# Four vision layers on one Trainium2 core: the selective scan under a written order of slots, with the exponentials in SBUF and the skip term on TensorE

## Chip, cores and metric

One core of a Trainium2 chip. The metric is the device time of one launch in microseconds (us). The engines are called PE (matrix multiplication), DVE (vector), ACT (activation functions), POOL (general purpose) and SP, which here only issues DMAs. All data is fp32.

## What is computed

Four layers run one after the other on 8 images of 384 channels and 32 x 32 pixels (1024 tokens): a Mamba block (layer 0), a Mamba block with a channel gate and an MLP (layer 1), seven depthwise convolutions merged into one 13 x 13 (layer 2), and a pointwise plus a depthwise convolution with GELU (layer 3). The change touches the Mamba block, which both layers 0 and 1 call. Its core, cut from the reference:

```python
u = silu(conv1d(xin) + conv_b)                      # 768 channels, 4 taps
dt_lo, Bm, Cm = split(u @ x_proj_w.T)               # 24, 16 and 16 columns
delta = softplus(dt_lo @ dt_proj_w.T + dt_proj_b)   # the step sizes
def step(h, inp):                                   # h: 768 channels x 16 states
    dt_t, u_t, B_t, C_t = inp
    dA = jnp.exp(dt_t[..., None] * A)
    h = h * dA + (dt_t * u_t)[..., None] * B_t[:, None, :]
    y = jnp.einsum('bdn,bn->bd', h, C_t)
    return (h, y)
...
y = ys + u * D                                      # the skip term
y = y * silu(z)
out = y @ out_proj_w.T                              # and the residual x is added
```

## The kernel before

**Tiling.** `mamba` walks over 16 units: image b = 0 to 7, half 0 or 1 of its 1024 tokens (T = 512 tokens). The 768 channels are six chunks d of 128. The scan has 16 states a channel, so a chunk has 2048 rows of 512 tokens; a tile of 128 partitions holds 32 channels x 4 states, and a work item handles two such tiles. Eight items (n = 0 to 7) make a chunk, 48 a unit, 768 a layer. Half 1 starts its scans from the `state` that half 0 left.

**One item** (`scan`, L273 to L295). POOL multiplies `B` (spread over the partitions) with `ur`, the repeated step size times u, into `dbu` in SBUF (L278; three buffers). ACT writes two exponentials of 512 columns into `h`, a tile in PSUM (L284; two buffers). DVE runs two scans of 512 columns over them (L288): each reads the exponentials from `h` and the addends from `dbu` and writes its result over `h`. In half 0 a small copy saves the last column (L290). DVE multiplies both with `C` into `hc` in SBUF (L292), and PE folds the states with two narrow matmuls of a 0/1 matrix into `acc` in PSUM (L295).

**The end of a chunk.** DVE forms `u * D + acc` (L296) and multiplies it with `zs`, the silu of z, from SBUF (L297).

**Step sizes.** `step_in` and `step_out` (L235 to L267) make delta and delta * u of a chunk: PE (L238), five passes on ACT, three on POOL (L253, L254, L256) and one on DVE (L255). Both tiles are written to DRAM (`dd`, `uu`) and read back repeated four times over the partitions, in eight DMAs of 128 KB for each (L265, `rdd`, `ruu`, three buffers each). They are issued inside the loop one chunk ahead: the step sizes of chunk d + 1 in items 0 and 1 of chunk d.

**The other work of a unit** is put into the items' places too (`fill`, L333 to L358): the gates z of this unit; the load, layer norm, input products, convolution (four diagonal products, L197) and silu of the next one; then its `ranks` (L216), which write B and C to DRAM and read them back spread. `back` (L299) forms the output products and adds the residual, in layer 1 after a gate on POOL (L307).

**Order.** Only ACT runs in the order that is written (`manual_schedule(engines={ACT})`, L317). The order on PE, DVE, POOL and SP is chosen by the scheduler of the language from the data dependences and its own estimates. A tile with n buffers makes its writer wait until the readers of the n-th tile before are through. Each engine runs its own queue strictly in order.

Of the kernel before, what the change touches and what calls it, by code (L numbers as in the profile page):

```python
# [9 lines left out]
F32 = mybir.dt.float32  # L10
AF = mybir.ActivationFunctionType
ALU = mybir.AluOpType
# [82 lines left out]

def mamba(tc, k, src, dst, w, v, gated):

    nc = tc.nc  # L100
    ACT = mybir.EngineType.Activation
    with ExitStack() as st:
# [3 lines left out]
        ps_mm = st.enter_context(tc.tile_pool(name="m_mm", bufs=3, space=PSUM))  # L106
        ps_y = st.enter_context(tc.tile_pool(name="m_y", bufs=1, space=PSUM))
        ps_da = st.enter_context(tc.tile_pool(name="m_da", bufs=2, space=PSUM))
# [4 lines left out]
        w_xp = wp.tile([P, KD, 32 + 2 * NS], F32, name="w_xp")  # L113
# [9 lines left out]
        carry = wp.tile([P, KD, 3], F32, name="carry")  # L123
# [16 lines left out]
        taps = wp.tile([P, KD, 4, P], F32, name="taps")  # L140
        for d in range(KD):
            for j in range(4):
                nc.gpsimd.tensor_scalar_mul(taps[:, d, j], k["ident"], conv_w[:, 4 * d + j : 4 * d + j + 1])

# [4 lines left out]
        def load(i):  # L149
            b, half = divmod(i, L // T)  # L150
            xt = work.tile([P, KC, T], F32, tag="xt", name="xt")
            nc.sync.dma_start(xt, src[b].rearrange("(c p) t -> p c t", p=P)[:, :, half * T : (half + 1) * T])
            return dict(i=i, b=b, half=half, xt=xt, us=[None] * KD, zs=[None] * KD, steps={}, ps={})

        def centre(s):
            xt = s["xt"]
            mean = ps_mm.tile([P, T], F32, tag="mm", name="mean")
            for c in range(KC):
                nc.tensor.matmul(mean, k["avg"], xt[:, c], start=c == 0, stop=c == KC - 1)
            nc.vector.tensor_tensor(xt, xt, mean.unsqueeze(1).to_broadcast([P, KC, T]), ALU.subtract)  # L160

        def squares(s):
            s["var"] = ps_mm.tile([P, T], F32, tag="mm", name="var")
            for c in range(KC):
                sq = work.tile([P, T], F32, tag="sq", name="sq")
                nc.scalar.activation(sq, s["xt"][:, c], AF.Square)
                nc.tensor.matmul(s["var"], k["avg"], sq, start=c == 0, stop=c == KC - 1)

        def rstd(s):

            y = work.tile([P, T], F32, tag="rs_y", name="rs_y", bufs=1)
            t = work.tile([P, T], F32, tag="rs_t", name="rs_t", bufs=1)
            u = work.tile([P, T], F32, tag="rs_v", name="rs_v", bufs=1)
            nc.scalar.activation(y, s["var"], AF.Ln, bias=k["eps"])
            nc.scalar.activation(u, s["var"], AF.Identity, bias=k["eps"])
            nc.scalar.activation(y, y, AF.Exp, scale=-0.5)
            nc.gpsimd.tensor_tensor(t, y, y, ALU.mult)
            nc.gpsimd.tensor_tensor(t, t, u, ALU.mult)
            nc.gpsimd.tensor_scalar(t, t, -0.5, 1.5, ALU.mult, ALU.add)
            nc.gpsimd.tensor_tensor(y, y, t, ALU.mult)  # L180
            nc.gpsimd.tensor_tensor(s["xt"], s["xt"], y.unsqueeze(1).to_broadcast([P, KC, T]), ALU.mult)  # L181

        def project(s, d):
            ps = ps_mm.tile([P, T], F32, tag="mm", name="ps_in")
            for c in range(KC):
                nc.tensor.matmul(ps, w_in[:, c, d * P : (d + 1) * P], s["xt"][:, c], start=c == 0, stop=c == KC - 1)  # L186
            xp = work.tile([P, T + 3], F32, tag="xp", name="xp")
            if s["half"] == 0:
                nc.gpsimd.memset(xp[:, 0:3], 0.0)
            else:  # L190
                nc.gpsimd.tensor_copy(xp[:, 0:3], carry[:, d])
            nc.scalar.activation(xp[:, 3:], ps, AF.Identity, bias=b_in[:, d : d + 1])  # L192
            if s["half"] == 0:
                nc.gpsimd.tensor_copy(carry[:, d], xp[:, T : T + 3])
            s["ps"][d] = ps_mm.tile([P, T], F32, tag="mm", name="ps_conv")
            for j in range(4):
                nc.tensor.matmul(s["ps"][d], taps[:, d, j], xp[:, j : j + T], start=j == 0, stop=j == 3)  # L197

        def silu_u(s, d):
            s["us"][d] = work.tile([P, T], F32, tag="u", name="u", bufs=12)  # L200
            nc.scalar.activation(s["us"][d], s["ps"].pop(d), AF.Silu, bias=conv_b[:, d : d + 1])

        def gate(s, d):
            ps = ps_mm.tile([P, T], F32, tag="mm", name="ps_z")
            for c in range(KC):
                nc.tensor.matmul(  # L206
                    ps, w_in[:, c, DI + d * P : DI + (d + 1) * P], s["xt"][:, c], start=c == 0, stop=c == KC - 1
                )
            s["zs"][d] = ps

        def silu_z(s, d):
            z = work.tile([P, T], F32, tag="zs", name="zs", bufs=4)
            nc.scalar.activation(z, s["zs"][d], AF.Silu, bias=b_in[:, KD + d : KD + d + 1])
            s["zs"][d] = z

        def ranks(s):  # L216

            ps = ps_mm.tile([P, T], F32, tag="mm", name="ps_xp")
            n = 32 + 2 * NS
            for d in range(KD):  # L220
                nc.tensor.matmul(ps[:n], w_xp[:, d], s["us"][d], start=d == 0, stop=d == KD - 1)
            dbc = work.tile([n, T], F32, tag="dbc", name="dbc")
            nc.scalar.activation(dbc, ps[:n], AF.Identity, bias=k["one_at_R"][:n])
            bc = dram.tile([2 * NS, T], F32, tag="bc", name="bc")
            nc.sync.dma_start(bc, dbc[32:n])
            s["dbc"] = dbc
            s["B"], s["C"] = [], []
            for g in range(4):
                for key, at in (("B", 0), ("C", NS)):
                    t = work.tile([P, T], F32, tag=key, name=key, bufs=6)  # L230
                    states = bass.AP(bc.tensor, bc.offset + (at + 4 * g) * T, [[T, 4], [0, 32], [1, T]])
                    nc.sync.dma_start(t, states)
                    s[key].append(t)

        def step_in(s, d):  # L235

            ps = ps_mm.tile([P, T], F32, tag="mm", name="ps_dt")
            nc.tensor.matmul(ps, w_dt[:, d * P : (d + 1) * P], s["dbc"][: R + 1], start=True, stop=True)  # L238
            e = work.tile([P, T], F32, tag="sp_e", name="sp_e")
            nc.scalar.activation(e, ps, AF.Abs)  # L240
            nc.scalar.activation(e, e, AF.Exp, scale=-1.0)
            s["steps"][d] = ps, e

        def step_out(s, d):
            ps, e = s["steps"][d]
            one = work.tile([P, T], F32, tag="sp_w", name="sp_w", bufs=1)
            lw = work.tile([P, T], F32, tag="sp_l", name="sp_l", bufs=1)
            delta = work.tile([P, T], F32, tag="delta", name="delta")
            du = work.tile([P, T], F32, tag="du", name="du")
            nc.scalar.activation(one, e, AF.Identity, bias=k["one"])  # L250
            nc.scalar.activation(lw, e, AF.Ln, bias=k["one"])
            nc.scalar.activation(one, one, AF.Identity, bias=k["minus"])  # L252
            nc.gpsimd.tensor_tensor(one, one, e, ALU.subtract)  # L253
            nc.gpsimd.tensor_tensor(lw, lw, one, ALU.subtract)  # L254
            nc.vector.scalar_tensor_tensor(delta, ps, 0.0, lw, ALU.max, ALU.add)  # L255
            nc.gpsimd.tensor_tensor(du, delta, s["us"][d], ALU.mult)  # L256
            got = []
            for key, t in (("dd", delta), ("uu", du)):
                flat = dram.tile([P, T], F32, tag=key, name=key)
                nc.sync.dma_start(flat, t)  # L260
                for h in range(2):
                    rep = work.tile([P, 2, T], F32, tag=f"r{key}", name=f"r{key}", bufs=3)
                    for q in range(4):
                        quarters = bass.AP(flat.tensor, flat.offset + 64 * h * T, [[T, 32], [32 * T, 2], [1, T]])
                        nc.sync.dma_start(rep[32 * q : 32 * q + 32], quarters)  # L265
                    got.append(rep)
            s["steps"][d] = got  # L267

        def scan(s, d, fill):
            half, u, acc = s["half"], s["us"][d], None  # L270
            dr, ur = s["steps"][d][:2], s["steps"][d][2:]
            acc = ps_y.tile([P, T], F32, tag="acc", name="acc")
# [496 lines left out]
```

## Time and profile before

| what | us |
|---|---|
| median of three runs (lowest, highest) | 11196.06 (11195.9, 11207.51) |
| the profiled execution | 11195.08 |
| its span, first to last instruction | 11192.9 |
| DVE busy in the span | 6525.3 (58%) |
| PE busy | 8208.6 (73%) |
| POOL busy | 4882.6 (44%) |
| ACT busy | 4186.9 (37%) |
| first to last scan, layer 0 | 139 to 4031 |
| first to last scan, layer 1 | 4625 to 8546 |
| mean granted PE clock | 0.816 of full speed |

Between the two layers stands the pooling for the channel gate, after the second the MLP, and from 9937 us on the convolutions, where PE is nearly always busy. In the profile a line names the line of the program (L288), the engine, the operation, the tile it writes and those it reads (`h<-h,dbu`), and the shape. "Idle before" is the time in which the engine stood idle just before such instructions, and what released them. Waiting that happens inside a running instruction has no row of its own: it is counted as busy and shows as a longer duration. Busy shares over the whole span mix the stages, so those of a Mamba stretch alone are to be read.

### The profile page before, as it was taken

To read this page: it belongs to the slowest core of one execution; us is meant where nothing else is said; L and a number is where in the kernel's file an instruction comes from. 1 tells how busy PE (TensorE), PEld (TensorE's weight loads), DVE (VectorE), ACT (ScalarE), POOL (GpSimd) and SP (SyncE) were. 2 spreads that over 40 slices of the span, in tenths; PEclk is the share of its full clock that TensorE was granted. 3 is DMA by queue.
4 is the path that set the end of the run, shared out by engine and by line. 5 is a ranking of instruction groups with operands and counts; after the bars stand their busy time and mean duration, and the time that the engine had idled before them with its cause. 6 is when DMAs were issued, how large, how long until landed. Compare 5 with 4: busy or idle time off the path is not lost.

```text
span 11192.9 us, 70040 instructions
## 1 busy us (share of the span) xinstructions
PE 8208.6 (73%) x20604; PEld 3067.5 (27%) x20604; DVE 6525.3 (58%) x6608; ACT 4186.9 (37%) x6006; POOL 4882.6 (44%) x2870
## 2 busy tenths in 40 slices
PE   6766677777667655676666777766766888889999
PEld 2111111111111111211111111111111333358688
DVE  4777777877777853477777787777775101010100
ACT  3444444444444422344444444444442212210100
POOL 4555565555556520455566556665663000001011
PEclk8877787877778666788787778777777999989999
DMA  2323333323333210233332323323322000034454
GB/s 77 83 81 86 86 82 82 82 80 82 88 86 82 79 54 28 66 84 83 86 84 77 84 80 82 86 79 85 85 80 63 17 19 21 15 61 84 130 84 79
DMA packets 964385, 825.81 MB, mean 74 GB/s; under 512 B 601458, under 2 KB 614898, under 8 KB 962980
## 3 DMA queue, kind: packets, MB, share of 16 engines
q1 hardware_dynamic: 834724, 758.39, 26.1%
q10 hardware_dynamic: 120064, 37.76, 1.3%
q0 software_dynamic: 9216, 25.18, 1.0%
q8 instruction: 165, 2.70, 0.1%
q14 instruction: 216, 1.77, 0.1%
HBM read 640.19 MB, written 180.82 MB: 73 GB/s over the span
## 4 chain that ended last, share of the span: by engine, by line
PE 23%; DVE 16%; issue 8%; POOL 6%; ACT 4%; DMA 1%; SPq 0%; DVEq 0%; POOLq 0%; ACTq 0%
DVE h L288 10%; PE ps L523 10%; PE ps_fc L454 5%; DVE hc L292 5%; PE ps_fc L459 4%; POOL dbu L278 3%; ACT h L284 2%; PE ps L559 1%; POOL sp_w L253 1%; POOL sp_l L254 1%; PE var L86 1%; PE acc L295 1%; ACT sp_w L250 0%; POOL xt L181 0%; PE mean L80 0%
## 5 line engine op out<-in xcount | busy, mean ns | idle before, releaser
L278 POOL TENSOR_TENSOR dbu<-B,ruu 128x1024 f32<-128x1024 f32 x1536 | 3593.2, 2355 | 683.7 <-DVE h L288 683.3
L295 PE MATMUL acc<-hc,fold 128*32 128x512 f32 x6144 | 2197.9, 803 | 2020.2 <-DVE hc L292 2018.1
L284 ACT ACTIVATE h<-rdd,A 128x512 f32<-128x512 f32 x3072 | 2115.8, 690 | 3279.9 <-DVE hc L292 3155.0
L288 DVE TENSOR_TENSOR_SCAN h<-h,state,dbu 128x512 f32<-128x512 f32 x1536 | 1938.9, 1281 | 407.9 <-POOL dbu L278 313.6
L288 DVE TENSOR_TENSOR_SCAN h<-h,dbu 128x512 f32<-128x512 f32 x1536 | 1867.2, 1225 | 371.5 <-POOL dbu L278 255.7
L292 DVE TENSOR_TENSOR hc<-h,C 128x1024 f32<-128x1024 f32 x1536 | 1867.7, 1216 | 36.0 <-DVE h L288 0.5
L295 PEld LDWEIGHTS acc<-hc,fold 128*32 128x32 f32 x6144 | 254.8, 121 | 3664.0 <-DVE hc L292 2857.2
L253 POOL TENSOR_TENSOR sp_w<-sp_w,sp_e 128x512 f32<-128x512 f32 x192 | 244.1, 1271 | 2113.7 <-ACT sp_w L252 2113.7
L523 PE MATMUL ps<-xp,wt 128*128 128x256 f32 x4992 | 1098.7, 382 | 19.5 <-DMA wt<-k_cols 19.5
L523 PEld LDWEIGHTS ps<-xp,wt 128*128 128x128 f32 x4992 | 942.6, 189 | 175.9 <-issue 20.6
L197 PE MATMUL ps_conv<-xp,taps 128*128 128x512 f32 x1536 | 864.1, 696 | 92.0 <-ACT xp L192 92.0
L310 PE MATMUL ps_out<-u,w_out 128*128 128x512 f32 x1152 | 711.3, 771 | 106.3 <-DVE u L297 100.9
L186 PE MATMUL ps_in<-xt,w_in 128*128 128x512 f32 x1152 | 678.4, 705 | 137.0 <-POOL xt L181 134.6
L518 POOL DMA_DIRECT2D xp<-x x192 | 169.7, 884 | 1299.7 <-PE ps L523 908.5
L206 PE MATMUL ps_z<-xt,w_in 128*128 128x512 f32 x1152 | 569.5, 627 | 124.5 <-DVE delta L255 69.1
L460 DVE SCALAR_TENSOR_TENSOR x<-ps_fc,vecs,x 128x512 f32<-128x512 f32 x48 | 36.0, 751 | 1019.3 <-PE ps_fc L459 1019.3
L454 PE MATMUL ps_fc<-xt,fc 128*128 128x512 f32 x1152 | 533.9, 628 | 126.8 <-ACT xt L93 126.8
L197 PEld LDWEIGHTS ps_conv<-xp,taps 128*128 128x128 f32 x1536 | 311.5, 222 | 723.8 <-issue 450.4
L447 POOL COPY xt<-x 128x1536 f32<-128x1536 f32 x16 | 23.5, 1467 | 1106.5 <-PE ps_fc L454 1095.1
L459 PE MATMUL ps_fc<-h,fc 128*128 128x512 f32 x1152 | 497.0, 592 | 0.0
L525 ACT ACTIVATE o<-ps,b_grp 128x256 f32<-128x256 f32 x192 | 90.9, 473 | 1001.5 <-PE ps L523 991.6
L296 DVE SCALAR_TENSOR_TENSOR u<-u,vecs,acc 128x512 f32<-128x512 f32 x192 | 143.5, 747 | 506.1 <-PE acc L295 506.1
(141 smaller groups left out, 6638.3 us busy)
## 6 DMA issues: line engine op xcount, KB each, us to landing
rdd<-dd SPq DMA_DIRECT2D x1536, 128.0 KB
ruu<-uu SPq DMA_DIRECT2D x1536, 128.0 KB
dd<-delta SPq DMA_DIRECT2D x192, 256.0 KB
uu<-du SPq DMA_DIRECT2D x192, 256.0 KB
wt<-k_cols SPq DMA_DIRECT2D x768, 52.0 KB
xt<-x SPq DMA_DIRECT2D x48, 768.0 KB
B<-bc SPq DMA_DIRECT2D x128, 256.0 KB
C<-bc SPq DMA_DIRECT2D x128, 256.0 KB
```

Source lines behind the costliest of these rows:

```text
L186: nc.tensor.matmul(ps, w_in[:, c, d * P : (d + 1) * P], s["xt"][:, c], start=c == 0, stop=c == KC - 1)
L197: nc.tensor.matmul(s["ps"][d], taps[:, d, j], xp[:, j : j + T], start=j == 0, stop=j == 3)
L206: nc.tensor.matmul(ps, w_in[:, c, DI + d * P : DI + (d + 1) * P], s["xt"][:, c], start=c == 0, stop=c == KC - 1)
L278: nc.gpsimd.tensor_tensor(dbu, s["B"][g].unsqueeze(1).to_broadcast([P, 2, T]), ur[h2], ALU.mult)
L284: nc.scalar.activation(h[:, q], dr[h2][:, q], AF.Exp, scale=A[:, a : a + 1])
L288: nc.vector.tensor_tensor_scan(h[:, q], h[:, q], dbu[:, q], first, ALU.mult, ALU.add)
L292: nc.vector.tensor_tensor(hc, h, s["C"][g].unsqueeze(1).to_broadcast([P, 2, T]), ALU.mult)
L295: nc.tensor.matmul(acc[32 * r : 32 * r + 32], k["fold"], hc[:, q], start=g == 0, stop=g == 3)
L310: nc.tensor.matmul(ps, w_out[:, d, m * P : (m + 1) * P], us[d], start=d == 0, stop=d == KD - 1)
L454: nc.tensor.matmul(ps, w1[:, c, m * P : (m + 1) * P], xt[:, c], start=c == 0, stop=c == KC - 1)
L459: nc.tensor.matmul(ps, w2[:, f, m * P : (m + 1) * P], h[:, f], start=f == 0, stop=f == KF - 1)
L523: nc.tensor.matmul(ps, wt[:, j], xp[:, :, j : j + HW], start=j == 0, stop=j == KS - 1)
```

## The change

It rewrites `mamba` between the preparation of the weights and the end; nothing else is touched.

- Every piece of work is a small function that is put into a numbered slot of a `Plan`; one slot stands for one item of the scan. The order on ACT, DVE, POOL and PE is the written one; only SP's is left to the scheduler.
- In slot K the loop issues the exponentials and `dbu` of item K + 2 (`before`), the two scans and `hc` of item K (`scan`), in even slots the folds of the two items before (`fold`), then what the plan holds for slot K.
- The exponentials go to a tile `a` in SBUF (three buffers); the scan reads `a` and `dbu`, both in SBUF, and writes `h` in PSUM, which has one buffer.
- Items alternate between the halves of a chunk (`g, h = divmod(n, 2)`).
- The skip term is a product on PE: `skip`, a diagonal matrix of D, times u opens the sum in `acc` (six more products a unit). The last step of a chunk is then one operation on DVE, `acc * zs`, a slot after the last fold.
- The step sizes of a chunk are worked out from 13 to 7 slots ahead of its first item; the repeated tiles are requested at 8, 7 and 3 slots ahead. The next unit's work is spread over the slots, products for z included, in groups of three for silu.
- The copies of the convolution's carried columns and the gate on the residual go from POOL to ACT; the scaling of the layer norm is split into three on POOL.
- PSUM: five buffers for products instead of three; one for `h` instead of two. Several SBUF tiles have one buffer instead of two.

```diff
-        ps_da = st.enter_context(tc.tile_pool(name="m_da", bufs=2, space=PSUM))
+        ps_h = st.enter_context(tc.tile_pool(name="m_h", bufs=1, space=PSUM))
...
+            nc.vector.tensor_scalar_mul(skip[:, d], k["ident"], D[:, d : d + 1])
...
+        def before(item):
+            i, d, n = item
+            s, (g, h) = units[i], divmod(n, 2)
+            a = work.tile([P, 2, T], F32, tag="a", name="a", bufs=3)
+            for q in range(2):
+                at = (d * 4 + 2 * h + q) * 4 + g
+                nc.scalar.activation(a[:, q], s.dr[d][1][h][:, q], AF.Exp, scale=A[:, at : at + 1])
+            dbu = work.tile([P, 2, T], F32, tag="dbu", name="dbu", bufs=3)
+            nc.gpsimd.tensor_tensor(dbu, s.B[g].unsqueeze(1).to_broadcast([P, 2, T]), s.ur[d][1][h], ALU.mult)
+            ready[item] = a, dbu
...
+            y = ps_h.tile([P, 2, T], F32, tag="h", name="h")
+            for q in range(2):
+                first = 0.0 if s.half == 0 else state[:, d, 2 * h + q, g : g + 1]
+                nc.vector.tensor_tensor_scan(y[:, q], a[:, q], dbu[:, q], first, ALU.mult, ALU.add)
...
+            if g == 0:
+                s.acc[d] = ps_y.tile([P, T], F32, tag="acc", name="acc")
+                nc.tensor.matmul(s.acc[d], skip[:, d], s.us[d], start=True, stop=False)
...
-            nc.vector.scalar_tensor_tensor(u, u, D[:, d : d + 1], acc, ALU.mult, ALU.add)
-            nc.vector.tensor_tensor(u, u, s["zs"][d], ALU.mult)
+        def y_out(s, d):
+            nc.vector.tensor_tensor(s.us[d], s.acc.pop(d), s.zs[d], ALU.mult)
...
+            for d in range(KD):
+                at = i * SLOTS + (d - 2) * PER
+                for e, f in ((3, sp_in), (4, sp_exp), (5, sp_ln), (6, sp_one), (7, sp_back), (8, sp_delta), (9, sp_du)):
+                    put(at + e, f, s, d)
+                put(at + 8, repeat, s, d, "d", 0)
+                put(at + 9, repeat, s, d, "u", 0)
+                put(at + 13, repeat, s, d, "d", 1)
+                put(at + 13, repeat, s, d, "u", 1)
+                put(at + 25, y_out, s, d)
...
-        with tc.manual_schedule(engines={ACT}):
+        with tc.manual_schedule(engines={E.Activation, E.DVE, E.Pool, E.PE}):
             exp_ln()
...
+            for K in range(-SLOTS - 3, n_items + 1):
+                if 0 <= K + 2 < n_items and K + 2 > 2:
+                    before(item(K + 2))
+                elif K == 0:
+                    for j in range(3):
+                        before(item(j))
+                if 0 <= K < n_items:
+                    scan(item(K))
+                if K > 0 and K % 2 == 0:
+                    fold([item(K - 2), item(K - 1)])
+                plan.run(K)
+            plan.rest()
```

## The prediction

> **What bounds the kernel now.** I read the table of stages first: the two Mamba layers (first to last scan 139 to 4031 and 4625 to 8546 us) hold seven tenths of the span. One stretch of them, busy time and number of instructions of each engine:
>
> ```profile
> core 0: us, PE busy (x) PEld busy (x) DVE busy (x) ACT busy (x) POOL busy (x), PEclk, DMA share, GB/s
> 1400.00:2520.00 1120.00, 793.17 (x1776) 209.04 (x1773) 887.66 (x858) 527.37 (x750) 664.28 (x376) 0.80 0.30 82
> ```
>
> DVE is the fullest engine, 79%. By the timeline the first scans of unit 0 and unit 15 start at 139.4 and 3815.8 us, and at 4625.3 and 8328.6 in the second layer: 245.1 and 246.9 us a unit, mean 246.0, or 5.13 for each of its 48 items. The waits of DVE (us in total, times, longest) say what it lacks:
>
> ```profile
> DVE h L288 <- POOL dbu L278: 569.3, 194, 10.3
> DVE u L296 <- PE acc L295: 506.1, 190, 6.1
> ...
> DVE h L288 <- ACT h L284: 174.5, 85, 4.4
> ```
>
> Over 32 units that is 17.8 + 15.8 + 5.5 = 39 us of each unit, nearly all at chunk ends, where `acc` and the next chunk's step sizes are late. So DVE works about 207 us a unit and waits 39. What an item costs (busy total, mean ns):
>
> ```profile
> L278 POOL TENSOR_TENSOR dbu<-B,ruu 128x1024 f32<-128x1024 f32 x1536 | 3593.2, 2355 | 683.7 <-DVE h L288 683.3
> ...
> L288 DVE TENSOR_TENSOR_SCAN h<-h,state,dbu 128x512 f32<-128x512 f32 x1536 | 1938.9, 1281 | 407.9 <-POOL dbu L278 313.6
> L288 DVE TENSOR_TENSOR_SCAN h<-h,dbu 128x512 f32<-128x512 f32 x1536 | 1867.2, 1225 | 371.5 <-POOL dbu L278 255.7
> L292 DVE TENSOR_TENSOR hc<-h,C 128x1024 f32<-128x1024 f32 x1536 | 1867.7, 1216 | 36.0 <-DVE h L288 0.5
> ```
>
> **The row that decides.** Last I took shortest, median and longest of single groups:
>
> ```profile
> L288 DVE TENSOR_TENSOR_SCAN h<-h,dbu x1536: 1204/1222/1232, 139.4 to 8308.1; 128x512 f32<-128x512 f32 x192
> L288 DVE TENSOR_TENSOR_SCAN h<-h,state,dbu x1536: 1258/1281/1294, 383.2 to 8545.0; 128x512 f32<-128x512 f32 x192
> ```
> ```profile
> L292 DVE TENSOR_TENSOR hc<-h,C x1536: 1199/1216/1226, 142.9 to 8546.3; 128x1024 f32<-128x1024 f32 x192
> ```
> ```profile
> L297 DVE TENSOR_TENSOR u<-u,zs x192: 691/1224/2810, 182.3 to 8550.4; 128x512 f32<-128x512 f32 x192
> ```
>
> The scans and `hc` run beside POOL's `dbu` most of the time and never stretch; each reads one tile from PSUM (`h`) and one from SBUF. L297 reads both from SBUF, and stretches from 0.69 to 2.81 us. The timeline shows how, first POOL, then DVE:
>
> ```profile
> 1028.62 1.26 POOL L254 TENSOR_TENSOR sp_l<-sp_l,sp_w 128x512 f32<-128x512 f32 x1
> ```
> ```profile
> 1028.97 1.46 DVE L297 TENSOR_TENSOR u<-u,zs 128x512 f32<-128x512 f32 x1
> ```
>
> POOL ends at 1029.88 and L297 at 1030.43, 0.55 later: it did not slow down, it stood still until POOL was through, and only 0.14 of its 0.69 us lay beside POOL. The same happens to POOL: an L297 that ends at 1165.73 us is followed by the end of a `sp_l`, issued at 1165.14, at 1166.85, 1.12 later instead of 1.27. After the change the scan (L347) reads `a` and `dbu`, both in SBUF, where it read `h` in PSUM. Every scan is then in L297's place, and every `dbu` beside it.
>
> **Parts that save.** Step sizes two chunks ahead and the written order take away what the 39 us waited for: `dbu` and `a` are made two items ahead, `acc` is read a slot after its last fold. The diagonal product turns L296 and L297 (0.747 + 1.185) into one operation with `acc` in PSUM, like L314 (0.689): 6 x 1.24 = 7.5 us of DVE a unit. It adds 6 matmuls, 0.47 each (six of L206 take 2.84), beside PE's idle time: PE is busy 71% of a stretch, and 3 us more of 246 hide. `carry` and the gated bias go from POOL to ACT, busy 47%; fewer table loads (1.28 each) likewise. DMAs are the same number; `rd`/`ru` are issued two slots before POOL needs them, some 10 us, and in a burst 2 to 3 MB moved in 24 us (145 GB/s), 7 us for the 1 MB of a half chunk. Where these covers fail, the wait comes back, at most the 39 us it was. By itself all this would give the first rival.
>
> **The part that costs, by one item.** `dbu`, `a` have three buffers, so `dbu` for two items ahead is freed by the second scan of the item before, and starts then: a scan that began at 1043.31 and took 1.29 let `dbu` start here:
>
> ```profile
> 1044.74 2.36 POOL L278 TENSOR_TENSOR dbu<-B,ruu 128x1024 f32<-128x1024 f32 x1 [0.85 <-DVE h L288]
> ```
>
> that is 0.14 later. It runs 2.35 us. Beside it DVE does `hc` (1.22; half-0 items also 0.16 for `state`, and at times 0.7 of `delta`, `u` or `o`), which costs nothing. Then the first scan stands until `dbu` ends and needs 1.25 - 0.14 = 1.11 more; the second follows, 1.30 (the pair at 1177.29 takes 2.49, the one at 1046.48 2.62; less the first, mean of both halves). Sum 0.14 + 2.35 + 1.11 + 1.30 = 4.90 us, 235.2 a unit.
>
> POOL's other work comes on top, since it can no longer lie beside a scan, and `hc`'s time is already taken by `dbu`: 18 `sp_w`, `sp_l`, `du` at 1.27, four steps of `rs` (1.04, 1.27, 0.62, 1.27) and three of `xt` at about 1.27, less 0.15 each as seen at `sp_l`: 20.2 + 3.6 + 3.4 = 27.2 us. Each stands between two scans and hides 0.14 of the one behind it: 24 or 25 of them, -3.4. `centre` (1.76) with `hc` outlasts `dbu` by 0.5 once. Unit: 235.2 + 27.2 - 3.4 + 0.5 = 259.5 us, 13.5 over 246.0. Times 32: +432. The start of each layer goes through more products in series; I add 10 a layer. Against the profiled execution (11195.08, span 11192.9, 2.2 around it; the median is 11196.06, 1 us above) this is 11195 + 452 = 11647, rounded **11650**.
>
> The unknown price is the wait of one scan, bounded from below by L288 as it is (0; no gain either: L314 with a PSUM and an SBUF input takes 0.689 and L563 with two from SBUF 0.693) and from above by a whole `dbu` (L297's longest, 2.81, is 0.69 + 2.12). I take L297's manner, as the nearest row: same engine, two SBUF inputs, same neighbour.
>
> The Trainium skill, page "SBUF — State Buffer", section "Who interferes with whom", says that a Vector instruction with two SBUF inputs contends with a GpSimd instruction that reads SBUF, and that the second to issue fully blocks; L297 agrees (0.69 to 2.81 us), no run yet shows it for a scan. By this rule the sum is the 11650 above; without it, the 9550 of the next part. It speaks against giving the exponentials SBUF tiles.
>
> **Rivals.**
> - *The scan does not wait for POOL* (16%). For it: scans stand beside `dbu` untouched now. Against: they read one SBUF tile now. Items in just this order follow each other now and then without a wait (the pairs that start at 1177.29 and 1181.02 us): 3.73, say 3.75 for both halves. A unit is 180.0 + 13.8 (`u` and `delta` 6 x 0.69 each, `xt` 1.76, three `o` 2.2, 1.5 of gaps) = 193.8, POOL's 144 beside it. 52.2 x 32 = 1670 off, 20 for the starts on: **9550**. This is the other side; it decides from the point where a scan's mean stays at 1.3.
> - *It waits, but the handover is cheaper* (13%): `dbu` shows its start-up 0.15 and the 0.14 before it beside DVE, scans the same 0.15 to 0.18 less, 1.07 each. 2.2 + 2.14 + 0.48 of other POOL work = 4.82, 231 a unit, 10,740 at the end of this; 10,800 to 11,300, centre 11,100. The break-even, 246 a unit, is 0.28 us an item below my sum.
> - *It waits, and `dbu` falls out of step* (13%): where `ru` lands late, or ACT is behind by its two tables and three `silu` (4.5 us), POOL's `dbu` comes between the two scans and `hc` lies beside nothing: 1.22 more. For all items 48 x 1.22 = 58.6 a unit more, 13,520; for a quarter to half of them 12,100 to 12,600, centre 12,300. Against: after such a miss `dbu` is again freed by a second scan, and back in step.
>
> **How the numbers follow.** Forecast 58%, 11,300 to 12,100. Slower by over 0.2% (about what a measurement of this kernel can tell from no change): 58 + 13 = 71%. The cheap handover splits into 8 faster and 5 within; with the first rival faster is 24%. The range leaves out the first rival and the ends of the other two, 2% each: 10,950 to 12,600.
>
> **What would show it.** Right: L347's scans average 1.8 to 1.9 us, the first of a pair above 2 and ending about 1.1 after a `dbu`; `dbu` stays at 2.35; DVE looks 90% busy with almost no wait for POOL, PE or ACT; units 260 us apart. Wrong at once: scans at 1.22 to 1.28 and units near 195. Wrong in size: gaps of POOL before `dbu` for DMA or ACT, or `sp_w` and `du` at 1.27 (they should show 2 and more).

## The result, and the profile after

The changed kernel takes 11564.42 us (median of 4 runs, 11562.35 to 11566.57) against 11196.67 in the same comparison: ratio 1.0326, 95% interval 1.0308 to 1.0344. The forecast was 11650, range 10,950 to 12,600. The profiled execution has a span of 11563.6 us, 370.7 more than before.

The stretch that was shown of before, in the table of stages of the changed kernel (PE, PEld, DVE, ACT, POOL busy, clock, DMA share, GB/s):

```profile
1400.00:2520.00 1120.00, 708.67 (x1710) 200.09 (x1708) 1062.44 (x801) 466.48 (x729) 739.29 (x322) 0.75 0.29 80
```

DVE went from 79% to 95% busy, and handled 801 instructions where it had handled 858: it looks fuller and does less (some 26 of the 57 are missing because two operations of each chunk became one). Its waits (us in total, times, longest) no longer have `acc` or the exponentials among the long ones, and `dbu` only at the starts of the two layers:

```profile
DVE h L347 <- POOL dbu L337: 50.2, 4, 24.8
...
DVE u L368 <- PE acc L363: 4.0, 2, 2.0
```

The mean granted PE clock is lower, 0.787 for 0.816, but with 4.0 us of waits for `acc` in all, where there were 506.1, PE is not what holds DVE in the scans.

The lost time is inside the instructions. The groups of the page (busy total, mean ns):

```profile
L337 POOL TENSOR_TENSOR dbu<-B,ru 128x1024 f32<-128x1024 f32 x1536 | 3675.5, 2393 | 2810.5 <-DVE h L347 2490.7
...
L347 DVE TENSOR_TENSOR_SCAN h<-a,dbu 128x512 f32<-128x512 f32 x1536 | 2767.7, 1802 | 200.9 <-POOL dbu L337 50.2
L347 DVE TENSOR_TENSOR_SCAN h<-a,state,dbu 128x512 f32<-128x512 f32 x1536 | 2777.2, 1808 | 152.0 <-ACT a L335 2.4
L351 DVE TENSOR_TENSOR hc<-h,C 128x1024 f32<-128x1024 f32 x1536 | 1873.8, 1220 | 72.1 <-DVE h L347 2.7
```

The scans went from 1225 and 1281 to 1802 and 1808 ns, in all 1739 us; `hc`, with one SBUF input, stayed. Shortest, median, longest of the same line show that the operation itself is no slower, most simply stand (2223 of the 3072 take over 1.3 us):

```profile
L347 DVE TENSOR_TENSOR_SCAN h<-a,dbu x1536: 1222/2032/3360, 130.9 to 8654.6; 128x512 f32<-128x512 f32 x192
L347 DVE TENSOR_TENSOR_SCAN h<-a,state,dbu x1536: 1283/2032/3411, 389.2 to 8903.9; 128x512 f32<-128x512 f32 x192
```

Where they stand is seen in the timeline, DVE first and then POOL, over one item without other POOL work:

```profile
2075.56 1.23 DVE L351 TENSOR_TENSOR hc<-h,C 128x1024 f32<-128x1024 f32 x1
2076.92 3.54 DVE L347 TENSOR_TENSOR_SCAN h<-a,state,dbu 128x512 f32<-128x512 f32 x2
2080.56 1.23 DVE L351 TENSOR_TENSOR hc<-h,C 128x1024 f32<-128x1024 f32 x1
```
```profile
2075.60 2.37 POOL L337 TENSOR_TENSOR dbu<-B,ru 128x1024 f32<-128x1024 f32 x1 [2.63 <-DVE h L347]
2080.60 2.37 POOL L337 TENSOR_TENSOR dbu<-B,ru 128x1024 f32<-128x1024 f32 x1 [2.63 <-DVE h L347]
```

`dbu` runs from 2075.60 to 2077.97, `hc` beside it. The pair of scans starts at 2076.92 and takes 3.54 us, where a pair alone took 2.62. The first ends at 2079.06, 1.09 after `dbu`. Of all scans in this trace that begin with at least 0.3 us of a `dbu` left, 1479, every one ends 1.085 to 1.098 us after it; in the kernel before 1344 scans began so and took 1.20 to 1.29 us as always. POOL in turn is idle 2.63 us until the second scan frees a buffer: neither engine is at work the whole item, they take turns.

### The profile page after: what moved, and what is told of

Same layout as the page of the kernel before. It is cut to its first block, busy times and chain, and to the rows that moved or that the text cites. A ratio compares the mean times of both kernels' runs of the same rounds, so it can differ in the third digit from the quotient of the medians.

```text
span 11563.6 us, 72598 instructions
## 1 busy us (share of the span) xinstructions
PE 7940.9 (69%) x20988; PEld 3100.0 (27%) x20988; DVE 8126.7 (70%) x6430; ACT 4016.7 (35%) x6222; POOL 5533.2 (48%) x2598
## 4 chain that ended last, share of the span: by engine, by line
DVE 49%; PE 29%; ACT 12%; issue 7%; DMA 3%; SPq 1%; DVEq 1%; POOL 0%; ACTq 0%; POOLq 0%
DVE h L347 42%; PE ps L626 10%; ACT a L335 9%; PE ps_fc L557 5%; PE ps_fc L562 4%; DVE hc L351 4%; PE mm L382 2%; DMA rd<-dd 1%; PE var L86 1%; PE ps L662 1%; PE mean L80 1%; PE acc L363 1%; SPq L324 1%; PE ps_lg L497 1%; ACT zs L258 1%
## 5 line engine op out<-in xcount | busy, mean ns | idle before, releaser
L337 POOL TENSOR_TENSOR dbu<-B,ru 128x1024 f32<-128x1024 f32 x1536 | 3675.5, 2393 | 2810.5 <-DVE h L347 2490.7
L335 ACT ACTIVATE a<-rd,A 128x512 f32<-128x512 f32 x3072 | 2048.3, 714 | 4473.0 <-DVE h L347 4450.0
L363 PE MATMUL acc<-hc,fold 128*32 128x512 f32 x6144 | 1824.3, 842 | 1806.5 <-DVE hc L351 1805.7
L347 DVE TENSOR_TENSOR_SCAN h<-a,dbu 128x512 f32<-128x512 f32 x1536 | 2767.7, 1802 | 200.9 <-POOL dbu L337 50.2
L347 DVE TENSOR_TENSOR_SCAN h<-a,state,dbu 128x512 f32<-128x512 f32 x1536 | 2777.2, 1808 | 152.0 <-ACT a L335 2.4
L234 PE MATMUL mm<-xt,w_in 128*128 128x512 f32 x2304 | 1192.1, 663 | 18.4 <-POOL xt L228 18.4
L360 PE MATMUL acc<-u,skip 128*128 128x512 f32 x384 | 366.1, 1053 | 1186.6 <-DVE u L368 1186.6
L247 PE MATMUL mm<-xp,taps 128*128 128x512 f32 x1536 | 746.7, 630 | 50.5 <-ACT xp L240 50.5
L234 PEld LDWEIGHTS mm<-xt,w_in 128*128 128x128 f32 x2304 | 474.8, 214 | 792.2 <-issue 717.1
L382 PE MATMUL mm<-u,w_out 128*128 128x512 f32 x1152 | 530.9, 611 | 0.0
```

The costliest lines, as they stand in the source:

```text
L234: nc.tensor.matmul(ps, w_in[:, c, m * P : (m + 1) * P], s.xt[:, c], start=c == 0, stop=c == KC - 1)
L247: nc.tensor.matmul(s.ps[d], taps[:, d, j], s.xp[:, j : j + T], start=j == 0, stop=j == 3)
L335: nc.scalar.activation(a[:, q], s.dr[d][1][h][:, q], AF.Exp, scale=A[:, at : at + 1])
L337: nc.gpsimd.tensor_tensor(dbu, s.B[g].unsqueeze(1).to_broadcast([P, 2, T]), s.ur[d][1][h], ALU.mult)
L347: nc.vector.tensor_tensor_scan(y[:, q], a[:, q], dbu[:, q], first, ALU.mult, ALU.add)
L360: nc.tensor.matmul(s.acc[d], skip[:, d], s.us[d], start=True, stop=False)
```

## The experiments

Unit times are the mean distance of the first scans of units 0 and 15, both layers: 246.0 us before, 256.2 after. The experiments e1, e2, e5 and e6 were run once each, the others four times.

**Without `dbu` (e1).**

```diff
+        still = wp.tile([P, 2, T], F32, name="still")
+        nc.vector.memset(still, 0.01)
...
-            dbu = work.tile([P, 2, T], F32, tag="dbu", name="dbu", bufs=3)
-            nc.gpsimd.tensor_tensor(dbu, s.B[g].unsqueeze(1).to_broadcast([P, 2, T]), s.ur[d][1][h], ALU.mult)
-            ready[item] = a, dbu
+            ready[item] = a, still
```

> The changed kernel without POOL's dbu product: the scans read one constant SBUF tile in its place, so the output is not the layer's; everything else, the a tiles in SBUF and the written order, is kept. My theory (a scan with both inputs in SBUF stands still while POOL's instruction runs): the scans go back to 1.22 to 1.28 us except where they meet POOL's 25 small operations a unit (scan mean at most 1.45), a unit takes 194 to 221 us, 9550 to 10,400 in all, estimate 9900. Rival one (a scan reading two SBUF tiles is slow by itself) and rival two (the written order with its single h buffer costs the time): scans stay at 1.8 us and the kernel at 11,560.

Measured: 10,268.39 us, 216.0 a unit, scans 1.38 in the mean, with medians of 1.23 in half 0 and 1.29 in half 1. Reading two SBUF tiles is not slow by itself, and the order and the single `h` are all still there: both rivals fall. The estimate of 9900 was too low. 16% of the scans are still longer than 1.4 us: nearly every one of POOL's small operations meets a scan (190 of the 192 `du` have one begin beside them, which ends 1.09 after).

**The scan's first input from PSUM (e2).**

```diff
+        held = ps_h.tile([P, 2, T], F32, tag="h", name="h")
+        nc.vector.memset(held, 0.5)
...
-            y = ps_h.tile([P, 2, T], F32, tag="h", name="h")
+            y = held
...
-                nc.vector.tensor_tensor_scan(y[:, q], a[:, q], dbu[:, q], first, ALU.mult, ALU.add)
+                nc.vector.tensor_tensor_scan(y[:, q], y[:, q], dbu[:, q], first, ALU.mult, ALU.add)
```

> The changed kernel, but the scan reads as its first input the PSUM tile it writes, with what the item before left there, instead of a; the exponentials are still made on ACT and read by nobody, so the output is not the layer's. POOL's dbu stays in full. My theory: one SBUF input is not held up, scans at 1.22 to 1.28 us beside a dbu of 2.35, units of 194 us, 9550 to 9700. The rival that POOL's product delays DVE whatever the scan reads, and the one that puts it to the order or the single h buffer: 11,560 and scans at 1.8.

Measured: 9797.39 us, 200.5 a unit. `dbu` is complete and as long as ever (median 2.36), and 1495 scans begin beside it; shortest, median and longest of all scans of this kernel:

```profile
L349 DVE TENSOR_TENSOR_SCAN h<-h,dbu x1536: 1219/1231/1232, 131.4 to 6937.6; 128x512 f32<-128x512 f32 x192
L349 DVE TENSOR_TENSOR_SCAN h<-h,state,dbu x1536: 1280/1291/1294, 327.1 to 7139.0; 128x512 f32<-128x512 f32 x192
```

Not one stands. One operand's place, with nothing else of DVE's or POOL's work changed, is worth 1767 us. (The scans no longer wait for ACT's `a` either, but in the changed kernel those waits come to 6.4 us in all.) The time lies 97 above the band I gave: an item takes 3.93 us in half 0 and 4.05 in half 1 (medians), where I had counted 3.75. With the one `h` buffer a scan starts 0.10 after the end of the `hc` before it; in the next run, with two, it starts 0.08 before that end, and the items take 3.73 and 3.85.

**All of the change but the SBUF tiles (e3).** The exponentials go back into `h` (two buffers), are made one item ahead (`decay`) and scanned in place; to find the PSUM for it, three buffers serve the products instead of five, and some slots move. ACT and POOL also take the last step of `delta` (0.68 us a chunk) from DVE.

```diff
-        ps_h = st.enter_context(tc.tile_pool(name="m_h", bufs=1, space=PSUM))
+        ps_h = st.enter_context(tc.tile_pool(name="m_h", bufs=2, space=PSUM))
...
+        def decay(item):
...
+            y = ps_h.tile([P, 2, T], F32, tag="h", name="h")
...
+                nc.scalar.activation(y[:, q], s.dr[d][1][h][:, q], AF.Exp, scale=A[:, at : at + 1])
...
+                nc.vector.tensor_tensor_scan(y[:, q], y[:, q], dbu[:, q], first, ALU.mult, ALU.add)
...
+            nc.scalar.activation(s.r, s.sp.pop(d), AF.Relu)
+            nc.gpsimd.tensor_tensor(s.delta, s.r, s.l, ALU.add)
```

> All of the changed kernel but the exponentials, which go into the PSUM tile h again (two buffers, one item ahead) and are scanned in place; three PSUM buffers for the products instead of five, so the slots of the input products, silu and z are moved, ACT takes max(x, 0) of the step sizes out of PSUM at once and POOL adds it. My theory: nothing of DVE is held up, about 190 us a unit (3.75 an item plus 10), 9400 to 9700 us, so 13 to 16% below the kernel before. Rival (the written order itself is what slows): 11,200 or more. If ACT's tables or POOL's extra addition bind, units of 200 to 215 us and 9750 to 10,200.

Measured: 9736.12 us, ratio to the kernel before 0.8696 (0.8682 to 0.8711), 198.8 a unit. This version beats both kernels. DVE over the same stretch, at 93%, is now at work:

```profile
1400.00:2520.00 1120.00, 838.42 (x2241) 250.90 (x2240) 1038.13 (x994) 674.31 (x1012) 832.53 (x439) 0.83 0.36 101
```

994 instructions instead of 801 at nearly the same busy time. The written order is not what slowed the changed kernel; with the other parts of the change it is worth 13%. The band was missed by 36 us: five chunks of a unit take 30 to 33 us, the first about 41.

**The SBUF tiles alone, on the kernel before (e5).**

```diff
+                a_sb = work.tile([P, 2, T], F32, tag="a", name="a", bufs=2)
...
-                    nc.scalar.activation(h[:, q], dr[h2][:, q], AF.Exp, scale=A[:, a : a + 1])
+                    nc.scalar.activation(a_sb[:, q], dr[h2][:, q], AF.Exp, scale=A[:, a : a + 1])
...
-                    nc.vector.tensor_tensor_scan(h[:, q], h[:, q], dbu[:, q], first, ALU.mult, ALU.add)
+                    nc.vector.tensor_tensor_scan(h[:, q], a_sb[:, q], dbu[:, q], first, ALU.mult, ALU.add)
```

> The kernel before with one part of the change alone: the exponentials go to an SBUF tile a (two buffers, since SBUF has no room for three; hc gets two as well) and the scan reads it, order and all else as before. My theory: at least 5.0 us an item (240 us a unit) plus what is left of the 39 us of waits at the chunk ends, 256 to 300 us a unit, 11,600 to 13,000, estimate 12,400, scans at 1.7 us or more. Rival (the new order makes the changed kernel slow, not the tiles): unchanged at 11,200 with scans at 1.25.

Measured: 12,683.56 us, 293.3 a unit, scans 1.79, inside the band. So the tiles cost about 1490 us in the old order (some of it may be the third `hc` buffer, which had to go), and the rest of the change gives 1120 of it back. The written order and the rest with the exponentials in PSUM is -1462 us, the tiles in SBUF +1828 on top of that, together the +368 of the result but for 2.

**Twelve of POOL's small operations fewer (e4).** The kernel lacks the rounding correction of the logarithm.

```diff
-            nc.gpsimd.tensor_tensor(s.w, s.w, s.e, ALU.subtract)
...
-            nc.gpsimd.tensor_tensor(s.l, s.l, s.w, ALU.subtract)
+            pass
```

> The changed kernel without two POOL subtractions of each chunk (the rounding correction of the logarithm, L298 and L301), 12 of the 25 small POOL operations of a unit; the output lacks that correction. My theory (POOL and the scans take turns, so every POOL operation adds to the unit): by the changed kernel's own rows, where an item without a small operation takes 5.00 us and one with takes 5.37 to 5.73, it is 12 x 0.4 to 0.7 = 5 to 9 us a unit less, 160 to 280 us, 11,280 to 11,400; by the 0.99 each of my sum 380 us, 11,180. Rival (POOL, busy 66% of a unit, has room, and what holds the scans is something else): no change, 11,564.

Measured: 11,317.49 us, ratio to the kernel before 1.0107 (1.0092 to 1.0122), 248.9 a unit: 247 us less than the changed kernel, 7.3 a unit or 0.61 for each of the twelve. POOL is idle a third of the time, and yet its small operations make the unit longer: the rival falls. The size is that of the rows, not the 0.99 of my sum.

**POOL writes but does not read (e6).**

```diff
-            nc.gpsimd.tensor_tensor(dbu, s.B[g].unsqueeze(1).to_broadcast([P, 2, T]), s.ur[d][1][h], ALU.mult)
+            nc.gpsimd.memset(dbu, 0.01)
+            nc.gpsimd.memset(dbu, 0.01)
```

> The changed kernel with POOL's dbu product replaced by two memsets of the same SBUF tile: POOL still works about 1.9 us an item (128 columns took 0.21, 3 columns 0.10) and writes as many tiles, but reads nothing; the output is not the layer's. Theory (it is POOL's reading that holds the scan, as the Trainium skill's SBUF page says): scans at 1.23 to 1.30 beside a memset, time as without dbu, 10,200 to 10,400. Rival (any POOL instruction holds a scan with two SBUF inputs): units of 235 us and more, 10,900 to 11,300, scans at 1.6 us or more.

Measured: 10,427.01 us, 220.9 a unit, 27 above the band but far from the rival's. 1017 scans begin with at least 0.3 us of a memset left, and take 1.23 to 1.30 us. POOL in the timeline of this kernel:

```profile
2004.43 0.95 POOL L337 MEMSET dbu<- 128x1024 f32 x1 [1.15 <-DVE h L348]
2005.44 0.95 POOL L338 MEMSET dbu<- 128x1024 f32 x1
2006.36 1.76 POOL L301 TENSOR_TENSOR sp_l<-sp_l,sp_w 128x512 f32<-128x512 f32 x1
```
```profile
2005.83 3.37 DVE L348 TENSOR_TENSOR_SCAN h<-a,dbu 128x512 f32<-128x512 f32 x2
```

The first scan starts at 2005.83 in the middle of the second memset, which ends at 2006.39, and is through at 2007.07, 0.68 later, after its usual 1.23 us. `sp_l`, which reads, waits behind that scan (1.76 for 1.27) and makes the second one stand. So it is POOL's reading of SBUF that matters here, and a POOL instruction that only writes passes; the memset is the one such instruction that was tried.

**The diagonal product undone (e7).**

```diff
-                nc.tensor.matmul(s.acc[d], skip[:, d], s.us[d], start=True, stop=False)
...
-            nc.vector.tensor_tensor(s.us[d], s.acc.pop(d), s.zs[d], ALU.mult)
+            nc.vector.scalar_tensor_tensor(s.us[d], s.us[d], D[:, d : d + 1], s.acc.pop(d), ALU.mult, ALU.add)
+            nc.vector.tensor_tensor(s.us[d], s.us[d], s.zs[d], ALU.mult)
```

> The changed kernel with one part undone: no diagonal product, u * D + acc and the product with zs are again two operations of DVE, the second with both inputs in SBUF. My theory: beside hc the first hides under dbu (1.22 + 0.75 of 2.49), the second waits for dbu, then adds its 0.55 and what the next scan does not hide, 0.14: 0.65 to 0.8 a chunk, 125 to 155 us more, 11,690 to 11,720. Rival (DVE's work sets the pace): 1.24 a chunk, 240 us, 11,800. If it hides altogether: 11,564.

Measured: 11,712.18 us, ratio to the kernel before 1.0458 (1.0441 to 1.0476), 148 us over the changed kernel or 0.78 a chunk. The first of the two operations (0.74 us, one SBUF input) lies whole inside a `dbu` in 190 of 192 cases, and by the size of the loss costs next to nothing; the second, which reads two, begins beside a POOL instruction in 190 of 192 and adds to the line.

**Stores on ACT's queue (e8)**, an attempt to win the slow first chunk of the PSUM version: the store is issued a slot later, and `o` has three buffers.

```diff
-            nc.sync.dma_start(dst[s.b][m * P : (m + 1) * P, s.cols], s.o[m])
+            nc.scalar.dma_start(dst[s.b][m * P : (m + 1) * P, s.cols], s.o[m])
```

> The written order with the exponentials in PSUM, as in e3, and the stores of the output moved from SP's queue to ACT's, one slot after their addition, with three o buffers instead of two. In e3 the first chunk of each unit takes 41 us where the others take 30 to 33, and SP's queue shows rd and ru behind such stores. Theory: that stall goes, 8 to 10 us a unit, 9420 to 9500. Rival (the first chunk is late for B, C or POOL's work, not for the queue): 9736 as it was.

Measured: 9742.3 us, ratio 0.8699 (0.8686 to 0.8712), the same as without it, and the first chunk still takes 41 to 42 us. The theory of the queue falls. In the trace POOL waits there 5.12 us for ACT (which has itself waited 2.51 us for PE, until 1757.32, since PE was at the output products from 1751.01 to 1756.43):

```profile
1753.13 2.36 POOL L344 TENSOR_TENSOR dbu<-B,ru 128x1024 f32<-128x1024 f32 x1 [1.35 <-DVE h L353]
1760.61 1.27 POOL L300 TENSOR_TENSOR sp_w<-sp_w,sp_e 128x512 f32<-128x512 f32 x1 [5.12 <-ACT sp_w L299]
```

Earlier in the chunk `ru` lands late as well (377 us of POOL's waits in this run). In the mean of 30 units, the first chunk holds 3.8 us of DVE's work that the others do not have (`xt` and the three `o`); DVE waits 2.8 in it for the output products and 3.8 for `dbu`, and POOL 4.6 for `ru` and 4.7 for ACT. So the 41 us have several parts, and the queue of the stores is none of them; which of POOL's two waits holds up `dbu` was not tried, and stays open.

## Why the prediction was right, step by step

- *The row that decides.* L297 was the right row for the scan: the scans stand until POOL is through and need 1.09 us more (1.11 in the sum). The Trainium skill, page "SBUF — State Buffer", section "Who interferes with whom", says that a Vector instruction with two SBUF inputs contends with a GpSimd instruction that reads SBUF, not with one that only writes, and that the second fully blocks. The runs agree on all three: 1479 scans behind `dbu`, none of 1495 with one input in PSUM (e2), none of 1017 beside a memset (e6).
- *One item.* Summed to 4.90; an item without small POOL work takes 5.00 in half 1 (2075.60 to 2080.60) and mostly 4.92 or 4.93 in half 0, 4.95 in the mean of all. Its order is the predicted one: `dbu` 0.14 behind the second scan (2080.46 and 2080.60), `hc` under it, the two scans after it. What the sum lacked is a gap of 0.10 between the two scans, where I had taken 0.04 from pairs that read `h` in PSUM.
- *POOL's other work* is the mis-sized term: 24.3 us a unit with `centre`; what is left over 48 items is 256.2 - 48 x 4.95 = 18.6. In the item of `sp_w` at 2087.92, shown at the end, `sp_w` ends 1.05 after the first scan (1.12 in the sum), and the second scan ends 1.09 after it, where without `sp_w` a gap of 0.10 and a whole scan of 1.29 would stand: 0.74 more than an item of 5.00, where the sum has 0.98. Of 776 items with one such operation 622 take about 5.7. This is a cheaper handover, as in the second rival, but for the small operations alone. Twelve fewer gave 0.61 each (e4).
- *The unit*: 256.2 against 259.5, so +10.2 instead of +13.5; for the 30 units that have a next one behind them, 98 us of the error.
- *The last unit of each layer* was counted like the others, and that was wrong the other way. With no next unit to prepare, it took 214 and 216 us before (from its first scan to the start of its last), and 245 and 246 after: +31 and +29 instead of twice 13.5, 34 us more than the sum has.
- *The starts*: I added 20. The first scan comes 8.5 us earlier (130.9 for 139.4), the way from the last scan of layer 0 to the first of layer 1 is unchanged (595.2 and 594.7), and what follows the last scan is 11.8 longer (why was not looked into). The scans of the two layers, +201.0 and +166.9, make up the rest of the 370.7. So the starts gave 3 instead of 20. The three errors, -98, +34 and -17, are the 81 us between the sum and the profiled execution: the mechanism was right, but that the sum came so near is in part luck, since two errors went against each other.
- *Parts that save* did save: the waits at the chunk ends are gone (4.0 us for `acc` in all), and e3, with the exponentials in PSUM, shows 13% for all the parts together. The burst is misread, since 145 GB/s over 24 us are 3.5 MB; POOL's waits for `ru` came to 67 us in all. The diagonal product is worth 148 us in the changed kernel, not the 240 of DVE's time, since part of it lay under `dbu`.
- *The first rival's price*, 9550, was 190 to 250 too low by e2 and e3: in e2 an item takes 3.99 in the mean of the halves, not 3.75; in e3, with two `h` buffers, 3.79, and the first chunk of a unit waits for `dbu` and the output products.

## What to carry to other kernels

Before an operand moves from PSUM to SBUF, count the SBUF inputs of the DVE instruction that reads it, and look at what POOL does meanwhile: with two, each POOL instruction that reads SBUF and each such DVE instruction are to be added up on one line, and neither engine need be full for that line to be the bound. The profile shows it as longer busy times, not as waits, so compare the shortest with the median duration of one line, and the share of busy time with the number of instructions done. An order of work that is good can be hidden by such a line: undo the parts of a change one at a time before it is thrown away.

## What the runs showed of the hardware

- The two engines alternate. A POOL instruction that waits gets in between two scans of DVE that follow each other without any wait: at 2086.92 a pair of scans takes 4.27 us, with `sp_w` (2.18 for 1.27) in between.

```profile
2086.92 4.27 DVE L347 TENSOR_TENSOR_SCAN h<-a,state,dbu 128x512 f32<-128x512 f32 x2
```
```profile
2085.59 2.37 POOL L337 TENSOR_TENSOR dbu<-B,ru 128x1024 f32<-128x1024 f32 x1 [2.62 <-DVE h L347]
2087.92 2.18 POOL L298 TENSOR_TENSOR sp_w<-sp_w,sp_e 128x512 f32<-128x512 f32 x1
2091.32 2.35 POOL L337 TENSOR_TENSOR dbu<-B,ru 128x1024 f32<-128x1024 f32 x1 [1.22 <-issue]
```

- A turn costs less than the instruction alone: a scan of 1.22 to 1.29 us ends 1.09 after the POOL instruction it stood behind, so some 0.13 to 0.20 of it is hidden.
- Between two successive scans into one `h` tile that each read two SBUF tiles lies a gap of 0.10 us (1514 of 1536 pairs of the changed kernel); where the first input is `h` in PSUM, in the same single buffer, it is 0.03 to 0.04 (all 1536 pairs of e2).
